# Four-layer graph network on one core: layer 2's normalised rows made and turned one batch earlier, three small steps moved

## The chip, the cores and the metric

One core of a Trainium2 chip runs the whole computation as one launch. The metric is the device time of one execution in microseconds (us). The kernel before was timed in three runs; the median counts.

## The reference, cut to what matters

`x` has 32 batches of 512 rows with 128 features, and `adj` is one 512 x 512 matrix shared by all batches. Four layers follow each other; each normalises every row, clips it at zero and adds what it computes to `x`:

```python
# layer 0: a softmax over adj's non-zero pattern mixes the rows
h = jnp.maximum(_layernorm(x), 0.0); x = x + _L0_gnn_ref(h, adj, ...)
# layer 1: two hops along adj, relu(stack @ Theta1 + bias)
h = jnp.maximum(_layernorm(x), 0.0); x = x + _L1_gnn_ref(h, adj, adj, ...)
# layer 2 (h is H, and weights = adj * adj)
features = relu(H @ psi_w + psi_b)
messages = einsum('nm,bnd->bmd', weights, features)
hidden = relu(concat(messages, H) @ phi1_w + phi1_b)
x = x + hidden @ phi2_w + phi2_b
# layer 3: exp(8 * tanh(score / 8)) * adj, rows divided by their sums, times h, times v
h = jnp.maximum(_layernorm(x), 0.0); x = x + _L3_gnn_ref(h, adj, q, k, v)
```

## The kernel before, in words

`x` stays in SBUF for the whole run, as 16 pairs of batches (`xt[q]`, q = 0 to 15; batch n is half b of pair q = n // 2). Every layer needs the statistics of each row, then the normalised rows (`h`), then these rows turned so that features lie on the partitions (`hT`).

**Statistics.** `stats_steps` (L239) of one pair issues four `bn_stats` on VectorE (L245), one square root on ScalarE (L252 or L254), and a reciprocal and a small multiply on VectorE (L256, L257). `low_stats` (L261) does the same without ScalarE: four `bn_stats` (L269) and four small operations on GpSimd (L271 to L274).

**Normalised and turned rows in layers 2 and 3.** `chunk(layer, m)` (L1076) makes the normalised rows of batch m with four ScalarE activations (L1089). `turn_half(layer, m)` (L1092) turns 32 x 32 blocks of them on VectorE (L1098) into one half of the tile `hb`, a ring of two buffers that both layers share; with the second half of a pair it also issues four 128 KB stores from SyncE to a DRAM tile `d` (L1104). `fetch(layer, q)` (L1107) loads the pair back from `d` as `hT` (512 KB, L1112, a ring of four); SyncE's queue is in order, so a fetch waits there until the four stores have landed.

**Order.** The order of instructions on TensorE, VectorE, ScalarE and GpSimd is the order of the source: a manual schedule covers these four engines, and DMAs that are held keep their place on SyncE's queue. So the place of a call in the source is its place in each engine's queue.

**Layer 0's last round and layer 1.** `round0(r)` (L794) handles pairs A = 2r and C = 2r + 1 of layer 0. It spreads the statistics of earlier pairs (`own_a`, `own_c`, L846) between its matrix products. In the last round (r = 7) `own_c` is pair 13. `layer1` (L950) handles two pairs per round: `split_up` makes high, low and mid parts of `h` (`moving_parts`, L418: high on ScalarE L420, low on GpSimd L421, mid on VectorE L422), `first` multiplies them with `adj` (`p_x1T`, L405, copied by ScalarE at L407), `weighed` and `mix` follow. In its first round it makes the statistics of pairs 14 and 15 (L1051, L1062). `more(step)` (L1352) places the first chunks, turns, fetches and features of layer 2 at the end of layer 1; step 7 is the last.

**Layer 2** is the first loop of `layers_2_and_3` (L1252), over n = 0 to 31. In iteration n: `messages(n)` (`p_msgT`, L1138, 12 matmuls), a chunk of layer 3 from n = 7 on, a chunk of layer 2 for batch n + 6, the copy of `p_msgT` out of PSUM by VectorE (L1276), `biased(n)` on GpSimd (L1167), `features(n + 2)` (`p_feat`, L447, from `hT`; then VectorE L1126, ScalarE L1127 and L420, GpSimd L421, VectorE L422), `hidden(n - 1)` (`p_phi`, L1147 and L1148, then ScalarE L1149), then the turns of the chunks that the iteration before made, `updated(n - 2)` (`p_l`, L447, then VectorE L1157, and for the second batch of a pair its statistics), and in even iterations a fetch for the batches n + 4 and n + 5. Two more statistics (pairs 14 and 15) are made at n = 2 and 3.

**Layer 3** is the second loop. `key_parts(n)` (ScalarE L426, VectorE L427, GpSimd L428) must precede `queries(n)` (`p_query`, L1183, then ScalarE L432 and VectorE L433, L434). `scores(n)` makes four tiles `ex` with a tanh and an exp each on ScalarE (L1211, L1203) and a multiply by the mask, alternately on VectorE and GpSimd (L1205). `attended(n - 1)` (`p_av`, L1232) uses the tiles of the batch before.

The lines below are the source that the change touches:

Of the kernel before, what the change touches and what calls it, by code (L numbers as in the profile page):

```python
# [29 lines left out]
def kernel(  # L30
# [38 lines left out]
    B, N, D = x.shape  # L69
# [3 lines left out]
    NQ = B // 2  # L73
# [138 lines left out]
    def ln_stats(q, low=False):  # L212
        for _ in stats_steps(q, low):
            pass
# [46 lines left out]
    def low_stats(q):  # L261

        st = stats.tile([P, NT, 2, 3], F32, tag="bn", name=f"bn_{q}", bufs=4)
        sd = stats.tile([P, NT, 2], F32, tag="sd", name=f"sd_{q}", bufs=4)
        rs = stats.tile([P, NT, 2], F32, tag="rs", name=f"rs_{q}")
        sh = stats.tile([P, NT, 2], F32, tag="sh", name=f"sh_{q}")
        for k in range(NT):
            b, t = divmod(2 * k, NT)
            nc.vector.bn_stats(st[:, k].rearrange("p e s -> p (e s)"),  # L269
                               xt[q][:, b, t : t + 2, :].rearrange("p t f -> p f t"))  # L270
        nc.gpsimd.tensor_scalar(sd, st[:, :, :, 2], 1.0 / (D * LOW**2), EPS / LOW**2, OP.mult, OP.add)  # L271
        nc.gpsimd.tensor_scalar(sh, st[:, :, :, 1], -1.0, None, OP.mult)
        nc.gpsimd.tensor_tensor(rs, sd, minus_half, OP.pow)
        nc.gpsimd.tensor_mul(sh, sh, rs)  # L274
        shift[q] = sh.rearrange("p k e -> p (k e)")
        scale[q] = rs.rearrange("p k e -> p (k e)")
# [202 lines left out]
    def go(steps, n=99):  # L479
        for _ in range(n):  # L480
            if next(steps, steps) is steps:
                return
# [311 lines left out]
    def round0(r):  # L794
# [48 lines left out]
        more = r + 1 < NQ // 2  # L843
        nothing = iter(())
        stats_a, stats_c = ahead.get(A + 5, nothing), ahead.get(C + 5, nothing)
        own_a, own_c = own.pop(A - 2, nothing), own.pop(C - 2, nothing)  # L846
        for i, _ in enumerate(products(f"l0_{r}", by_token, sums["att"], now, evict,
                                          ORDER if r else ORDER0)):
            if r == 0:
# [100 lines left out]
    def layer1(more, square):  # L950
# [68 lines left out]
        for r in range(NQ // 2):  # L1019
            A, C = 2 * r, 2 * r + 1  # L1020
            last = r == NQ // 2 - 1
            if r == 0:
                first(A, 1)
                split_up(C, 0)
                split_up(C, 1)
                straighten(C)
            else:
                split_up(A, 1)
                straighten(A)
                mix(r - 1, 0)  # L1030
                normalised(C, NT)
                turn(C, 1)
                mix(r - 1, 1)
                normalised(C)
                turn(C)
                mix(r - 1, 2)
                split_up(C, 0)
                go(square, r > 3)
                mix(r - 1, 3)
                split_up(C, 1)  # L1040
                first(A, 1)
            weighed(A, 0)
            weighed(A, 1)
            if last:
                more(0)
            go(square, r > 2)
            first(C, 0)
            normalised(A + 2, NT)
            if last:
                more(1)  # L1050
            ln_stats(A - 2) if r else go(own[NQ - 2])  # L1051
            first(C, 1)
            if last:
                more(2)
            if r:
                straighten(C)
            split_up(A + 2, 0)
            normalised(A + 2)
            go(square, r > 3)
            weighed(C, 0)  # L1060
            weighed(C, 1)
            ln_stats(C - 2) if r else go(own[NQ - 1])  # L1062
            go(square, r > 3)
            turn(A + 2)
            first(A + 2, 0)
            if r == 0:
                normalised(C + 2, 0)
# [8 lines left out]
    def chunk(layer, m):  # L1076


        q, b = divmod(m, 2)
        if layer == 3 and m % 4 == 0:  # L1080
            h = wide_tile(f"h3_{m}")
            halves_h.update({(3, m + i): tiles(h[:, i]) for i in range(4)})
        elif layer == 2 and b == 0:
            h = normed_tile(q)
            halves_h.update({(2, m + i): h[:, i] for i in range(2)})
        h = halves_h[layer, m]
        for t in range(NT):
            i = b * NT + t
            nc.scalar.activation(h[:, t, :], xt[q][:, b, t, :], AF.Relu,  # L1089
                                 bias=shift[q][:, i : i + 1], scale=scale[q][:, i : i + 1])  # L1090
# [16 lines left out]
    def fetch(layer, q):  # L1107

        if q < NQ:
            hT = hTs[layer, q] = feature_major(f"hT{layer}_{q}")  # L1110
            tc.keep_in_program_order(
                nc.sync.dma_start(hT.rearrange("p i b n -> p (i b n)"), dh[layer, q].rearrange("j c i e -> (j c) (i e)")))  # L1112
# [38 lines left out]
    def updated(n):  # L1151

        if not 0 <= n < B:
            return
        q, b = divmod(n, 2)
        p = projected(f"p_l2_{n}", (columns(msgT[n // 4][:, n % 4]), phi2))
        nc.vector.tensor_add(xt[q][:, b], p, xt[q][:, b])  # L1157
        if b == 1 and q == NQ - 1:
            low_stats(q)
        elif b == 1:  # L1160
            ln_stats(q, low=True)

    def biased(n):
# [88 lines left out]
    def layers_2_and_3():  # L1252


        later, ready = iter(range(B)), []

        def ahead_of_3():
            m = next(later, B)
            if m < B:
                chunk(3, m)  # L1260
                ready.append((3, m))

        def turn_ready(now):
            for layer, m in now:
                turn_half(layer, m)

        mask_of = adjT_d.rearrange("(a b c) w -> b a c w", a=NT, c=QR)
        for n in range(B):
            p = messages(n)
            now, ready = ready, []  # L1270
            if 7 <= n < B - 1:
                ahead_of_3()
            if n + 6 < B:
                chunk(2, n + 6)
                ready.append((2, n + 6))
            nc.vector.tensor_scalar(msgT[n // 4][:, n % 4], p, UP, None, OP.mult)  # L1276
            biased(n)
            features(n + 2)
            if n == B - 1:
                queries(0)  # L1280
            hidden(n - 1)
            turn_ready(now)
            updated(n - 2)
            if n == 0:
                fetch(2, 2)
            elif n % 2 == 0 and n + 4 < B:
                fetch(2, n // 2 + 2)
            if n in (2, 3):
                ln_stats(NQ - 4 + n)
            if n == 12:  # L1290
                weights_of_3()
            if n == 20:
                adjTx.append(matrix_tile("adjTx"))
            if n >= 20 and n % 2 and n < 28:
                i = (n - 20) // 2
                tc.keep_in_program_order(nc.sync.dma_start(adjTx[0][:, i, :], mask_of[i]))
            if n in (26, 28, 30):
                fetch(3, (n - 26) // 2)
            if n in (29, 30):
                key_parts(n - 29)  # L1300
        hidden(B - 1)
        mapped(0)
        updated(B - 2)
        updated(B - 1)
        for n in range(B):
            last = n == B - 1
            queries(n + 1)
            key_parts(n + 2)
            if last:
                attended(n - 2, NT // 2)  # L1310
            else:
                scores(n)
                if n == B - 2:
                    attended(n - 1, 0, NT // 2)
                    mapped(n + 1)
                    scores(n + 1)
                    continue
            attended(n - 1)
            mapped(n + 1)
            if n % 2:  # L1320
                turn_ready(ready)
                ready = []
            elif n:
                ahead_of_3()
            if n % 2 == 0:
                fetch(3, n // 2 + 3)
        attended(B - 1, width=1)
# [24 lines left out]
    def more(step):  # L1352

        if step == 0:
            chunk(2, 0)
        elif step == 1:
            chunk(2, 1)
            turn_half(2, 0)
        elif step == 2:
            turn_half(2, 1)  # L1360
        elif step == 3:
            fetch(2, 0)
            chunk(2, 2)
        elif step == 4:
            turn_half(2, 2)
            chunk(2, 3)
        elif step == 5:
            turn_half(2, 3)
            features(0)
            chunk(2, 4)  # L1370
        elif step == 6:
            fetch(2, 1)
            features(1)
            turn_half(2, 4)
            chunk(2, 5)
        elif step == 7:
            turn_half(2, 5)

    next_layer = layer1(more, made_square)
    for r in range(NQ // 2):  # L1380
# [42 lines left out]
```

## Time and profile before

| quantity | value |
|---|---|
| median of 3 runs (lowest, highest) | 929.79 us (928.28, 930.12) |
| the profiled execution's own time | 931.19 us |
| its span, first to last instruction | 929.3 us |
| busy in the span: TensorE / VectorE / ScalarE / GpSimd | 906.4 / 668.5 / 527.7 / 488.0 us |
| mean granted TensorE clock | 0.996 of full speed |
| layer 2 in the span (first `p_msgT` to last `p_msgT` starts) | 452.28 us to 661.47 us |

The profiled execution is one of the program's executions; 1.9 us of its time lie outside the span. All durations below come from it. In the profile PE is TensorE's matrix multiply, PEld its weight load, DVE VectorE, ACT ScalarE, POOL GpSimd and SPq SyncE's queue, which issues the DMAs. In a line of the timeline the first number is the start from the beginning of the span, the second the length, both in us; xN says how many instructions are merged; a bracket at the end gives the idle time of the engine before it and what ended that.

### The profile page before, as it was taken

Reading aid. Unit: us, or ns where it says so; the run is one execution under the profiler, and the core shown is the slowest. Engines: PE = TensorE matmul, PEld = TensorE weight load, DVE = VectorE, ACT = ScalarE, POOL = GpSimd, SP = SyncE. Lnnn points to the kernel's source line nnn. Section 1 sums busy time; section 2 is a strip of 40 time slices with the busy share of each in tenths; the row PEclk is TensorE's granted clock in tenths of the full one; section 3 lists DMA queues with packets and bytes.
Section 4 is the critical chain, followed back from the end, with each engine's and each line's share of the span. In section 5 each row is a group of like instructions: output and inputs, shape, how many; then the busy total and the mean of one; then the engine's idle time right before and its main releaser. Section 6 shows DMA issues by size and latency. Waiting matters only on the chain.

```text
span 929.3 us, 15172 instructions
## 1 busy us (share of the span) xinstructions
PE 906.4 (98%) x5433; PEld 775.1 (83%) x5433; DVE 668.5 (72%) x1348; ACT 527.7 (57%) x1156; POOL 488.0 (53%) x435
## 2 busy tenths in 40 slices
PE   8999999999999999999998999999999999999998
PEld 4899999988888888888876766767789999999998
DVE  8888886666665665666575666666788888887775
ACT  5864553343452353344645776775487777766663
POOL 5968999732132245422444444444465665555553
PEclk9999999999999999999998999999999999999999
DMA  9255643113213302312312334346412232222111
GB/s 254 63 166 167 175 115 112 46 47 91 68 42 116 93 24 68 91 45 93 92 52 84 93 112 137 98 132 172 121 30 74 73 98 80 80 80 80 59 35 46
DMA packets 83915, 86.06 MB, mean 93 GB/s; under 512 B 6784, under 2 KB 74624, under 8 KB 83840
## 3 DMA queue, kind: packets, MB, share of 16 engines
q1 hardware_dynamic: 83552, 84.57, 31.8%
q8 instruction: 43, 0.70, 0.3%
q10 hardware_dynamic: 288, 0.52, 0.2%
q14 instruction: 32, 0.26, 0.1%
HBM read 44.17 MB, written 40.89 MB: 92 GB/s over the span
## 4 chain that ended last, share of the span: by engine, by line
PE 80%; DVE 5%; DMA 4%; POOL 4%; ACT 4%; issue 2%; SPq 1%; DVEq 0%; POOLq 0%; ACTq 0%
PE p_av L1232 12%; PE p_l L1003 10%; PE p_x1T L405 9%; PE p_score L1210 9%; PE p_w L447 6%; PE p_msgT L1138 4%; PE p_l_c L393 3%; PE p_l L999 3%; PE p_hv L447 3%; PE p_l_d L393 2%; PE p_g L447 2%; PE p_query L1183 2%; PE p_l_a L393 2%; ACT h L1089 2%; PE p_feat L447 2%
## 5 line engine op out<-in xcount | busy, mean ns | idle before, releaser
L421 POOL TENSOR_TENSOR low_feat<-feat,high_feat 128x512 fp32r<-128x512 f32 x32 | 56.5, 1767 | 131.9 <-ACT high_feat L420 131.4
L1232 PEld LDWEIGHTS p_av<-hv,ex 128*128 128x128 f32 x1024 | 119.2, 191 | 2.7
L1232 PE MATMUL p_av<-hv,ex 128*128 128x129 f32 x1024 | 119.4, 274 | 0.0
L285 ACT ACTIVATE h<-x,sh,rs 128x128 f32<-128x128 f32 x256 | 102.8, 483 | 12.5 <-DVE sh L257 11.5
L1205 DVE TENSOR_TENSOR ex<-ex,adjTx 128x512 f32<-128x512 f32 x64 | 82.5, 1289 | 34.9 <-ACT ex L1203 33.1
L1205 POOL TENSOR_TENSOR ex<-ex,adjTx 128x512 f32<-128x512 f32 x64 | 99.4, 1572 | 7.1 <-issue 4.2
L1089 ACT ACTIVATE h<-x,sh,rs 128x128 f32<-128x128 f32 x256 | 102.9, 484 | 0.0
L428 POOL TENSOR_TENSOR key<-key 128x512 fp32r<-128x512 f32 x32 | 50.3, 1570 | 94.4 <-DVE key L427 41.7
L421 POOL TENSOR_TENSOR low_h<-h,high_h 128x512 fp32r<-128x512 f32 x32 | 47.1, 1481 | 79.0 <-ACT high_h L420 78.8
L245 DVE BATCH_NORM_STATS2 bn<-x 128x6 f32<-128x256 f32 x244 | 85.8, 415 | 0.0
L407 ACT ACTIVATE x1T<-p_x1T 128x512 f32<-128x512 f32 x32 | 19.0, 594 | 106.8 <-PE p_x1T L405 106.8
L1203 ACT ACTIVATE ex<-ex 128x512 f32<-128x512 f32 x128 | 78.9, 651 | 0.0
L1211 ACT ACTIVATE ex<-p_score 128x512 f32<-128x512 f32 x128 | 74.0, 605 | 1.4 <-PE p_score L1210 1.3
L422 DVE SCALAR_TENSOR_TENSOR mid_feat<-feat,high_feat 128x512 fp32r<-128x512 f32 x32 | 24.4, 764 | 55.4 <-ACT high_feat L420 55.4
L432 ACT ACTIVATE high_query<-p_query 128x512 fp32r<-128x512 f32 x32 | 19.2, 600 | 73.1 <-PE p_query L1183 73.1
L974 POOL COPY hs<-hT 128x512 f32<-128x512 f32 x32 | 19.2, 630 | 79.0 <-DMA hT<-d_hT 78.9
L254 ACT ACTIVATE sd<-bn,eps 128x8 f32<-128x8 f32 x46 | 13.9, 302 | 64.5 <-DVE bn L245 61.4
L1210 PE MATMUL p_score<-low_query,key 128*128 128x512 f32 x128 | 50.4, 394 | 0.0
L1210 PE MATMUL p_score<-high_query,key 128*128 128x512 f32 x128 | 50.4, 394 | 0.0
L1210 PE MATMUL p_score<-mid_query,key 128*128 128x512 f32 x128 | 50.4, 394 | 0.0
L447 PEld LDWEIGHTS p_feat<-psi,hT 128*128 128x128 f32 x256 | 33.4, 195 | 19.4 <-issue 11.3
L447 PE MATMUL p_w<-th,x1T 128*128 128x128 f32 x256 | 49.5, 275 | 0.0
(220 smaller groups left out, 2370.2 us busy)
## 6 DMA issues: line engine op xcount, KB each, us to landing
d<-hb SPq DMA_DIRECT2D x128, 128.0 KB, 2.4
hT<-d SPq DMA_DIRECT2D x32, 512.0 KB, 3.7
d_hT<-hb_hT SPq DMA_DIRECT2D x112, 128.0 KB, 2.4
hT<-d_hT SPq DMA_DIRECT2D x28, 512.0 KB, 3.3
x<-in_x_dram SPq DMA_DIRECT2D x32, 256.0 KB, 5.3
out_dram<-x SPq DMA_DIRECT2D x31, 256.0 KB, 2.3
adjT_d<-adj_squares SPq DMA_DIRECT2D x4, 256.0 KB
adj_crossed<-in_adj_dram SPq DMA_DIRECT2D x4, 256.0 KB
```

Of the source, the lines that this page charges most:

```text
L245: nc.vector.bn_stats(st[:, k].rearrange("p e s -> p (e s)"), xt[q][:, b, t : t + 2, :].rearrange("p t f -> p f t"))
L285: nc.scalar.activation(h[:, b, t, :], xt[q][:, b, t, :], AF.Relu, bias=shift[q][:, i : i + 1], scale=scale[q][:, i : i + 1])
L405: nc.tensor.matmul(p, right[part][:, blk(t)], left[part][:, t, :], start=(t == 0 and part == 0), stop=(t == NT - 1 and part == 2))
L421: nc.gpsimd.tensor_sub(low, x, high.bitcast(F32))
L447: nc.tensor.matmul(p[:, blk(t)], hT(t), w, start=(i == 0), stop=(i == len(terms) - 1))
L1003: nc.tensor.matmul(p, adj_parts[part][:, t, blk(i)], w[r][part][:, t, :], start=False, stop=(part == 2 and t == NT - 1), skip_group_check= ...
L1089: nc.scalar.activation(h[:, t, :], xt[q][:, b, t, :], AF.Relu, bias=shift[q][:, i : i + 1], scale=scale[q][:, i : i + 1])
L1203: nc.scalar.activation(ex[:, t, :], ex[:, t, :], AF.Exp, scale=8.0)
L1205: eng.tensor_mul(split(ex[:, t, :]), split(ex[:, t, :]), crossed(mask[:, t, :]))
L1210: nc.tensor.matmul(p, keys[n][i][:, t, :], query[n][i], start=(i == 0), stop=(i == 2))
L1211: nc.scalar.activation(crossed(ex[:, t, :]), split(p), AF.Tanh, scale=UP / (8.0 * math.sqrt(D)))
L1232: nc.tensor.matmul(po[:, i, : D + 1], ex[:, t, blk(i0 + i)], hv[:, t, :], start=(t == 0), stop=(t == NT - 1))
```

## The change

Four things move; no arithmetic is added or removed.

1. Statistics of pair 13 leave layer 0's last round and go to layer 1's first round, just ahead of those of pair 14.
2. In layer 2, the chunk of batch n + 7 (instead of n + 6) is made in iteration n, the one of batch 6 in step 7 ahead of the loop. The turns of what the iteration before made are placed directly after `messages(n)`, ahead of the copy of `p_msgT`, instead of after `hidden(n - 1)`. The fetches, apart from the first, sit in odd iterations, one iteration earlier than before.
3. `key_parts(2)` goes from layer 3's first iteration to the end of layer 2, ahead of `hidden(31)`.
4. `low_stats` of pair 15 goes from `updated(31)` to layer 3's second iteration.

```diff
-        own_a, own_c = own.pop(A - 2, nothing), own.pop(C - 2, nothing)
+        own_a, own_c = own.pop(A - 2, nothing), own.pop(C - 2, nothing) if more else nothing
...
-            ln_stats(A - 2) if r else go(own[NQ - 2])
+            if r:
+                ln_stats(A - 2)
+            else:
+                go(own[NQ - 3])
+                go(own[NQ - 2])
...
-        if b == 1 and q == NQ - 1:
-            low_stats(q)
-        elif b == 1:
+        if b == 1 and q < NQ - 1:
             ln_stats(q, low=True)
...
-        later, ready = iter(range(B)), []
+        later, ready = iter(range(B)), [(2, 6)]
...
             p = messages(n)
-            now, ready = ready, []
+            turn_ready(ready)
+            ready = []
             if 7 <= n < B - 1:
                 ahead_of_3()
-            if n + 6 < B:
-                chunk(2, n + 6)
-                ready.append((2, n + 6))
+            if n + 7 < B:
+                chunk(2, n + 7)
+                ready.append((2, n + 7))
...
             hidden(n - 1)
-            turn_ready(now)
             updated(n - 2)
             if n == 0:
                 fetch(2, 2)
-            elif n % 2 == 0 and n + 4 < B:
-                fetch(2, n // 2 + 2)
+            elif n % 2 and n + 5 < B:
+                fetch(2, n // 2 + 3)
...
+        key_parts(2)
         hidden(B - 1)
...
-            key_parts(n + 2)
+            if n:
+                key_parts(n + 2)
+            if n == 1:
+                low_stats(NQ - 1)
...
             turn_half(2, 5)
+            chunk(2, 6)
```

## The prediction, made before the changed kernel ran

> **What bounds the kernel now.** I read the page first, then who waited for whom on TensorE, then windows by stage, then the timeline where TensorE stood still. The page's parts 1 and 2 show TensorE busy throughout, with one dip in slice 21 and in the granted clock a slice later:
>
> ```profile
> PE 906.4 (98%) x5433; PEld 775.1 (83%) x5433; DVE 668.5 (72%) x1348; ACT 527.7 (57%) x1156; POOL 488.0 (53%) x435
> ```
>
> The windows view says where the missing 23 us are (columns: length, then busy us of PE, PEld, DVE, ACT, POOL, then clock):
>
> ```profile
> 200.00:452.00 252.00, 252.00 (x1475) 219.69 (x1474) 154.52 (x279) 105.06 (x239) 79.88 (x78) 1.00 0.26 72
> 467.54:661.47 193.93, 180.77 (x892) 134.53 (x890) 129.50 (x257) 126.92 (x289) 88.98 (x85) 0.98 0.39 112
> 637.45:656.32 18.87, 18.87 (x98) 14.40 (x97) 11.94 (x23) 10.44 (x23) 9.59 (x10) 1.00 0.55 159
> ```
>
> Layer 1 (first row) has no idle TensorE at all. Layer 2 from messages(3) to messages(31) (second row) has 193.93 - 180.77 = 13.16 us, and a lowered clock. The third row is three iterations of layer 2 without a stall: 6.29 us each, the pace TensorE can hold. The waits of TensorE name one cause:
>
> ```profile
> PE p_feat L447 <- DMA hT<-d: 13.1, 10, 3.6
> ```
>
> Ten times `features` stood before a fetch that had not landed. The worst, on TensorE's timeline:
>
> ```profile
> 488.62 1.10 PE L1138 MATMUL p_msgT<-sq_mid,mid_feat 128*128 128x512 f32 x4
> 493.34 2.05 PE L447 MATMUL p_feat<-psi,hT 128*128 128x128 f32 x8 [3.62 <-DMA hT<-d]
> 495.18 1.91 PE L1147 MATMUL p_phi<-hT,phi 128*128 128x512 f32 x2
> 502.64 1.05 PE L447 MATMUL p_feat<-psi,hT 128*128 128x128 f32 x8
> ```
>
> After 3.62 us of idling the same eight matmuls took 2.05 us, later 1.05 us: half clock. Why are fetches late again and again? This part of the timeline is a stretch of the loop where neither TensorE nor a DMA is waited for:
>
> ```profile
> 507.71 1.42 DVE L245 BATCH_NORM_STATS2 bn<-x 128x6 f32<-128x256 f32 x4
> 509.17 0.30 ACT L252 ACTIVATE sd<-bn,eps_low 128x8 f32<-128x8 f32 x1 [2.78 <-DVE bn L245]
> 509.38 3.17 ACT L1089 ACTIVATE h<-x,sh,rs 128x128 f32<-128x128 f32 x8
> 509.82 0.68 DVE L1276 TENSOR_SCALAR msgT<-p_msgT 128x512 f32<-128x512 f32 x1
> 512.46 0.61 ACT L1127 ACTIVATE feat<-feat 128x512 f32<-128x512 f32 x1
> 514.43 1.30 DVE L1098 STREAM_TRANSPOSE hb<-h 128x512 f32<-128x512 f32 x2
> 519.58 1.30 DVE L1098 STREAM_TRANSPOSE hb<-h 128x512 f32<-128x512 f32 x2
> 521.38 1.40 DVE L245 BATCH_NORM_STATS2 bn<-x 128x6 f32<-128x256 f32 x4
> ```
>
> VectorE and ScalarE hand work to each other: statistics, square root, eight activations of the two chunks, then feat, its high part, the mid part, two turns, an add; then a lighter iteration. From statistics to statistics, two iterations, it takes 521.38 - 507.71 = 13.67 us, against TensorE's 2 x 6.29 = 12.58. The turns, hence stores and fetches, are paced by this loop. So two things bound layer 2: the loop's 13.67 us, and a fetch that leaves no spare time behind the turn.
>
> Two small idles lie elsewhere: 1.16 us before `mid_h` at 187.75, and
>
> ```profile
> 678.18 0.50 PE L1183 MATMUL p_query<-key,qk_parts 128*128 128x512 f32 x1 [1.20 <-POOL key L428]
> ```
>
> **What the Trainium skill says.** "TensorE: Matmul & The Clock Gate", section "What's actually happening", puts the clock at half after an idle window of about 3.4 us and back at full after about as much activity. The trace agrees: only the 3.62 us idle is followed by half clock; idles up to 1.61 us are not. "DMA: Bandwidth & Descriptors", section on the anatomy of one DMA, gives 2.0 us fixed plus bytes / 436 GB/s: an estimate of 2.3 us for a store and 3.2 for a fetch; the page's rows say 2.4 and 3.7 here (the measured ones are used). "SBUF — State Buffer", section "Who interferes with whom", says a VectorE instruction with two SBUF inputs and a GpSimd one lock each other out for a whole instruction. The trace agrees: the mid part takes 0.69 us, but 1.84 at 475.07, beside GpSimd's low part.
>
> **Part by part.**
>
> *Layer 2, what goes.* Stalled, messages(3) to messages(31) takes 193.93 us. Unstalled it is 27 x 6.29 + 5.39 (iteration 30 has no features; 656.08 to 661.47) = 175.22. Difference 18.71 us: 13.14 of idling, 3.2 of half clock (iteration 6 took 13.12 us, 6.83 too many, of which 3.62 are idle), and 2.3 of restarting after gaps.
>
> *Does the fetch come in time?* Chunk and turn are an iteration earlier. Before, a second-half turn sat in iteration 2k - 4 after the mid part; now it opens iteration 2k - 5, for the same features(2k) in 2k - 2. That is 6.3 us for the iteration plus 4.6 from VectorE's opening of an iteration to its turn (509.82 to 514.43): almost 11 us earlier, against a lateness of at most 3.62. Counted forward: turns 1.3, eight stores at 0.43 (the median row) 3.5, landing 2.4, fetch 3.7, together 11 us; VectorE opens an iteration 3.8 us behind TensorE (509.82 against messages at 506.06) and features come 2.9 us into one (508.95), so there are 3 x 6.29 + 2.9 - 3.8 = 18 us. The stall goes, and about 7 us are spare. Buffers: fetch of pair k takes the buffer of k - 4, last read by hidden in the iteration before; free.
>
> *What is late next: the loop.* The order of instructions shows each pair of turns passing the add and, in odd iterations, the statistics. The turns at 514.43 now come after the small multiply that ends the statistics (509.74 + 0.17), where ScalarE is busy with the eight activations until 512.46. VectorE's path there is 509.9 + 1.22 (turns) + 0.6 (copy) + 0.6 (feat) = 512.4: hidden, with 0.1 us to spare. The other turns, at 519.58, go ahead of the lighter iteration's copy and stay on the path. Loop: 13.67 - 1.22 = 12.45, under 12.58 by 0.13. So TensorE becomes the bound; but the cover is thin. If a lock of 1.84 - 0.69 = 1.15 us hits one mid part in every second loop, the loop averages 13.0, 0.45 too slow in each of the nine double iterations with both layers' chunks (n = 7 to 24): 4 us, less what the parts are ahead of TensorE's need: the relu of hidden at 513.64 is ready at 514.31 and used by `p_l` at 517.86, 3.5 us, of which I count 2. I take 1.0 us for this; bounds 0 and 4.
>
> *SyncE's queue.* Turns of layer 3 and layer 2 now complete a pair in the same odd iteration: eight stores instead of four and four, then the fetch. The next turns write the same `hb` buffers, so they wait for these stores. With the new order the light iteration's turns come at about 515.0 (mid 513.82, add 514.43), 5.1 after the others at 509.9; on to the next ones it is 12.45 - 5.1 = 7.3, and 0.6 more for the second buffer: 7.9 us. The last of the eight stores lands 0.7 + 3.5 + 2.4 = 6.6 after the turn began. No wait, 1.3 us spare.
>
> *Start of the loop.* Chunk(2,6) keeps its place on ScalarE (it merely changes iteration); chunk(2,7) is added ahead of feat(2) in ScalarE's 2.61 us of idling before 456.93: 1.64 us, hidden. Without that cover it would cost that.
>
> *Pair 13's statistics.* Four `bn_stats`, reciprocal and multiply leave the path before `mid_h`: VectorE is free at 185.2 (end of `x` from p_l_e) instead of 186.5. GpSimd's low part may still lock it until 186.6; gain 0.5 to 1.3, I take 1.1. Given back in layer 1: pair 14's square root now waits for pair 13's reciprocal and then its own `bn_stats`; ScalarE's square root moves from 200.20 to about 200.5 + 0.4 + 1.4 = 202.3, and behind it is queued the copy of `p_x1T` (200.85), which `p_w` needs at 202.66. New 202.6 + 0.6 = 203.2: a stall of 0.6. Net +0.5; bounds -0.5 and +1.2.
>
> *key_parts(2) and low_stats(15).* The 1.20 us go, but ScalarE's key part now sits before hidden(31)'s relu (0.1 to 0.3 us), and `p_av` at 681.30 had the last GpSimd tile of batch 0 ready at 681.53 only, used 0.3 us later: what starts earlier there is ScalarE's tanh and exp, by 0.3 to 0.6. In the next iteration `low_stats` puts 2.3 us of GpSimd (0.20 + 0.24 + 1.67 + 0.20) ahead of batch 1's tiles, which end at 687.5 against a use at 689.7. Net +0.3; bounds -0.8 and +1.2.
>
> *Sum:* 18.7 - 1.0 + 0.5 + 0.3 = 18.5. Of the profiled execution: 931.19 - 18.5 = 912.7. It lies 1.4 us over the median, so 929.79 - 18.5 = 911.3.
>
> **Rivals.**
> 1. *TensorE sets layer 2's pace* (as summed), 911.3; 908.5 to 913.5. For: hand-over loop shorter than 12.58, fetch 7 us early.
> 2. *The loop still sets the pace*, at 13.0 to 13.4 through locks: 9 x 0.4 to 0.8, less 2, is 1.6 to 5.2 us in place of case 1's allowance of 1.0: 912 to 915.5, about 914. For: 0.13 us of margin. Against: the stretch shown already has GpSimd's low part in it, with mid first.
> 3. *Features still wait for fetches* (the change doesn't do what it says), because SyncE's queue holds them behind the other stores: gains only the first stall, 6.8, and about nothing else: 923. Against: 7 us spare.
> 4. *Slower:* `hb` buffers come free late. If stores crowd, the turn blocks VectorE, with copy and feat queued behind it, and the loop is 12.45 plus the wait. To eat the 18.5 us in nine double iterations it must reach 12.58 + (18.5 + 1 + 2) / 9 = 15.0: a last store landing 7.9 + 2.5 - 4.2 = 6.2 us after its issue. At 6.7 us the loop is 15.5: 9 x 2.9 - 2 - 1 = 23 over case 1, 934. Against: the stores of `hb` landed in 2.0 to 3.4 us.
>
> **Numbers.** Chances: case 1 0.64, case 2 0.25, case 3 0.06, case 4 0.05. The range runs from 908.0 (all stalls gone, the small parts at their best: 18.7 + 1.2 + 1.2 = 21.1, 908.7, and some scatter) to 916.5 (case 2's end); it leaves out cases 3 and 4. A measurement of this kernel tells about 0.2% (1.9 us) from no change: faster is cases 1 to 3 and a little less, 0.93; same 0.02; slower 0.05.
>
> **What would show it.** Right: no `p_feat` wait for hT; no half clock near 490; messages 6.29 us apart from 467 to 661; turns between the multiply L257 and the copy of `p_msgT`. A new wait at the copy of `p_x1T` or `p_w` near 201.5, and a shorter one at the third batch's `p_query`. Wrong: pitch above 12.7 us per two iterations with TensorE waiting for low or mid feat (case 2), turns waiting for stores (case 4), or a half clock without idling.

## The result, and the profile after

| | before | after |
|---|---|---|
| median of the runs, timed together (lowest, highest) | 929.95 us (928.28, 930.22; 4 runs) | 912.73 us (912.55, 912.96; 4 runs) |
| ratio after / before, 95% interval | | 0.9819 (0.9802 to 0.9836) |
| profiled execution: time, span | 931.19, 929.3 us | 912.96, 911.2 us |
| mean granted TensorE clock | 0.996 | 1.000 |

The forecast was 911.3 us (908.0 to 916.5); for the profiled execution 912.7, which came out at 912.96. That the sum comes within 0.3 us there is luck. By the medians the kernel gained 17.2 us and not 18.5; the profiled execution of before was 1.2 us slower than the median of its runs. Nor do all terms of the sum hold; the sections below say which.

The first line of part 1 of the page of after:

```profile
PE 901.1 (99%) x5432; PEld 774.2 (85%) x5433; DVE 669.7 (74%) x1348; ACT 527.5 (58%) x1156; POOL 485.6 (53%) x435
```

The same instructions are there. TensorE is 5.3 us less busy, for no stretch runs at half clock and few matmuls restart after a gap; its idle time fell from 23 to 10 us. The windows of after (columns as before: length, busy us of PE, PEld, DVE, ACT, POOL, clock, share of the DMA engines, GB/s), first messages(3) to messages(31), then three unstalled iterations:

```profile
465.83:643.20 177.37, 176.03 (x891) 133.20 (x890) 132.70 (x255) 126.01 (x286) 88.59 (x86) 1.00 0.41 117
618.94:637.80 18.86, 18.86 (x99) 14.40 (x98) 12.67 (x25) 12.33 (x26) 9.67 (x10) 1.00 0.55 167
```

177.37 in place of 193.93: 16.56 of the 18.2 us come from here. It is still 2.15 us more than 27 iterations of 6.29 and one of 5.39. VectorE is 3.2 us *busier* than before in this stretch (132.70 against 129.50), though it does nearly the same work (255 instructions against 257). The waits of TensorE in after (us in total, times, longest):

```profile
PE p_l L447 <- ACT msgT L1153: 1.3, 2, 0.7
PE p_av L1234 <- POOL ex L1207: 0.8, 1, 0.8
...
PE p_w L447 <- ACT x1T L407: 0.3, 1, 0.3
```

The ten waits of `features` for `hT` are gone, and so are those at `mid_h` and `p_query`. Three small ones are new: `p_l` for the relu of `hidden`, `p_w` for the copy of `p_x1T`, and `p_av` for GpSimd's tile. (Waits in the first 20 us of the run, and one of 0.3 us that before has too, are left out here.) Now the loop between VectorE and ScalarE, on VectorE's timeline, two iterations from statistics to statistics:

```profile
501.44 1.41 DVE L245 BATCH_NORM_STATS2 bn<-x 128x6 f32<-128x256 f32 x4
503.22 0.20 DVE L256 RECIPROCAL rs<-sd 128x8 f32<-128x8 f32 x1 [0.37 <-ACT sd L252]
503.46 0.17 DVE L257 SCALAR_TENSOR_TENSOR sh<-bn,rs 128x8 f32<-128x8 f32 x1
503.64 1.30 DVE L1102 STREAM_TRANSPOSE hb<-h 128x512 f32<-128x512 f32 x2
504.87 0.65 DVE L1279 TENSOR_SCALAR msgT<-p_msgT 128x512 f32<-128x512 f32 x1
505.44 0.68 DVE L1130 TENSOR_TENSOR feat<-p_feat,psib 128x512 f32<-128x512 f32 x1
507.55 1.80 DVE L422 SCALAR_TENSOR_TENSOR mid_feat<-feat,high_feat 128x512 fp32r<-128x512 f32 x1 [1.43 <-ACT high_feat L420]
...
513.76 0.69 DVE L422 SCALAR_TENSOR_TENSOR mid_feat<-feat,high_feat 128x512 fp32r<-128x512 f32 x1 [1.42 <-ACT high_feat L420]
514.37 0.69 DVE L1161 TENSOR_TENSOR x<-p_l,x 128x512 f32<-128x512 f32 x1
514.97 1.42 DVE L245 BATCH_NORM_STATS2 bn<-x 128x6 f32<-128x256 f32 x4
```

The turns stand right behind the small multiply, as forecast, and ScalarE's eight activations (503.10 to 506.18) cover them. Yet the loop takes 514.97 - 501.44 = 13.53 us, not 12.45: one of the two mid parts takes 1.80 us in place of 0.69. GpSimd's low part of the same features says why:

```profile
507.54 1.27 POOL L421 TENSOR_TENSOR low_feat<-feat,high_feat 128x512 fp32r<-128x512 f32 x1 [4.11 <-ACT high_feat L420]
...
513.86 1.72 POOL L421 TENSOR_TENSOR low_feat<-feat,high_feat 128x512 fp32r<-128x512 f32 x1 [3.22 <-ACT high_feat L420]
```

Both engines wait for the same high part. At 507.54 GpSimd is 0.01 us ahead: its instruction runs undisturbed in 1.27 us, and VectorE's, which takes 0.69 alone, ends 0.54 us after it: VectorE was locked out for nearly all of GpSimd's instruction. At 513.76 VectorE is 0.10 us ahead: its instruction takes 0.69 and GpSimd's 1.72. How far VectorE has fallen behind (start of its copy of `p_msgT` less start of the same `messages`, worked out from the trace, us), and the mid part made in that iteration:

| iteration n | 6 | 8 | 10 | 12 | 14 | 16 | 20 | 24 |
|---|---|---|---|---|---|---|---|---|
| mid part | 1.83 | 1.80 | 1.81 | 1.81 | 0.69 | 0.69 | 0.69 | 0.69 |
| VectorE behind by | 7.10 | 7.49 | 8.43 | 9.36 | 9.58 | 8.16 | 7.62 | 7.08 |

While every loop has its lock, VectorE falls behind by 0.94 us in two iterations (13.52 - 12.58), until TensorE has to wait, at n = 13 and 15:

```profile
535.15 1.16 PE L447 MATMUL p_l<-phi,msgT 128*128 128x128 f32 x8 [0.63 <-ACT msgT L1153]
...
548.85 1.16 PE L447 MATMUL p_l<-phi,msgT 128*128 128x128 f32 x8 [0.72 <-ACT msgT L1153]
```

From n = 13 on VectorE is ahead by 0.045 us each time, no lock comes any more, and it catches up by 0.27 us in two iterations. The loop from n = 12 also holds a small operation that is done once for layer 3 (`qk_parts`, 0.30 us on VectorE); it takes 13.71 us.

My theory after this (theory L below): the place of the turns gave the gain, by taking them out of the hand-over loop; who wins the lock decides the 2.15 us left. The rivals: the earlier chunks and fetches gave the gain, since the fetch was issued too late (rival F), and the two stalls have another cause.

### The profile page after: what moved, and what is told of

Read it like the earlier page. It is cut to its first block, busy times and chain, and to the rows that moved or that the text cites. A ratio compares the mean times of both kernels' runs of the same rounds, so it can differ in the third digit from the quotient of the medians.

```text
span 911.2 us, 15170 instructions
## 1 busy us (share of the span) xinstructions
PE 901.1 (99%) x5432; PEld 774.2 (85%) x5433; DVE 669.7 (74%) x1348; ACT 527.5 (58%) x1156; POOL 485.6 (53%) x435
## 4 chain that ended last, share of the span: by engine, by line
PE 92%; ACT 3%; DVE 3%; POOL 1%; issue 0%; DMA 0%; DVEq 0%; POOLq 0%; ACTq 0%
PE p_av L1234 12%; PE p_l L1003 10%; PE p_x1T L405 9%; PE p_score L1212 9%; PE p_msgT L1142 9%; PE p_w L447 6%; PE p_l_c L393 4%; PE p_l L999 3%; PE p_l_a L393 3%; PE p_l_d L393 3%; PE p_g L447 3%; PE p_l L447 3%; PE p_hv L447 3%; PE p_feat L447 3%; PE p_phi L1151 3%; PE p_phi L1152 3%
## 5 line engine op out<-in xcount | busy, mean ns | idle before, releaser
L421 POOL TENSOR_TENSOR low_feat<-feat,high_feat 128x512 fp32r<-128x512 f32 x32 | 53.9, 1686 | 115.8 <-ACT high_feat L420 111.7
L1207 DVE TENSOR_TENSOR ex<-ex,adjTx 128x512 f32<-128x512 f32 x64 | 80.4, 1259 | 35.7 <-ACT ex L1205 34.0
L422 DVE SCALAR_TENSOR_TENSOR mid_feat<-feat,high_feat 128x512 fp32r<-128x512 f32 x32 | 28.9, 904 | 44.3 <-ACT high_feat L420 44.3
L447 PE MATMUL p_w<-th,hs 128*128 128x128 f32 x256 | 49.4, 275 | 0.0
```

Source lines behind the costliest of these rows:

```text
L421: nc.gpsimd.tensor_sub(low, x, high.bitcast(F32))
L447: nc.tensor.matmul(p[:, blk(t)], hT(t), w, start=(i == 0), stop=(i == len(terms) - 1))
L1207: eng.tensor_mul(split(ex[:, t, :]), split(ex[:, t, :]), crossed(mask[:, t, :]))
```

## Experiments

Where each kernel spends its time (us, worked out from the starts of instructions in the profiled executions; messages(0) to messages(3) is 15.25 to 15.30 in all):

| kernel | start to first `p_x1T` | to messages(0) | messages(3) to (31) | messages(31) to end | span |
|---|---|---|---|---|---|
| before | 184.19 | 268.09 | 193.93 | 267.85 | 929.3 |
| after | 183.61 | 266.97 | 177.37 | 267.98 | 911.2 |
| layer 2 undone | 183.59 | 266.96 | 193.30 | 267.77 | 926.9 |
| turns only | 183.72 | 266.94 | 176.38 | 267.80 | 910.1 |
| chunks and fetches only | 183.57 | 266.95 | 186.20 | 268.02 | 920.0 |
| layer 2 only | 186.28 | 267.64 | 177.36 | 267.80 | 914.3 |
| low part first | 183.58 | 267.15 | 192.95 | 270.20 | 929.2 |
| mid part first | 184.81 | 267.17 | 175.17 | 267.85 | 910.3 |
| pair 13 undone | 184.04 | 267.65 | 177.37 | 267.75 | 912.1 |
| key parts, pair 15 undone | 183.97 | 266.95 | 177.38 | 267.75 | 911.3 |
| two moves corrected | 183.58 | 266.35 | 177.37 | 266.89 | 909.5 |
| both corrected and mid first | 183.83 | 266.60 | 175.17 | 267.03 | 907.9 |

The first column varies by up to 2.7 us, in waits near the start that the edits do not touch (`p_incl` L530 waits 0.3 us in after and 1.3 in layer 2 only). So small effects are read from the columns, not from the totals. Each ratio below is to the kernel before, timed on the same chip.

**Layer 2 undone.** The layer 2 hunks of the diff reversed, the other three parts kept.

> The changed kernel with the layer 2 part alone put back as it was: turns after hidden(n - 1), chunks for batch n + 6, fetches in even iterations. My theory (the whole gain but 1 to 2 us is layer 2's): 928 to 929 us, ten waits of features for hT with about 13 us in all, one stretch at half clock. Rival (the small moves matter more, or the parts help each other): under 925.

Measured: 929.39 us median against 929.31, ratio 0.9998 (0.9991 to 1.0006). Ten waits for `hT` of 13.0 us in all are back. The median lies a little above the expected 928 to 929. The whole measurable gain is layer 2's; what the other parts bring is inside this measurement's uncertainty.

**Turns only.** The turns stay directly after `messages(n)`; chunks and fetches go back to where they were before.

```diff
-        later, ready = iter(range(B)), [(2, 6)]
+        later, ready = iter(range(B)), []
...
-            if n + 7 < B:
-                chunk(2, n + 7)
-                ready.append((2, n + 7))
+            if n + 6 < B:
+                chunk(2, n + 6)
+                ready.append((2, n + 6))
...
-            elif n % 2 and n + 5 < B:
-                fetch(2, n // 2 + 3)
+            elif n % 2 == 0 and n + 4 < B:
+                fetch(2, n // 2 + 2)
...
             turn_half(2, 5)
-            chunk(2, 6)
```

> The changed kernel with the turns directly after messages, but chunks for batch n + 6 and fetches in even iterations as before. Theory L (the hand-over loop of VectorE and ScalarE was the bound, and the place of the turns shortens it): the turn comes 4.6 us earlier than before, which leaves 18.0 - 6.3 = 11.7 us up to the features against 1.3 + 4 x 0.43 + 2.4 + 3.7 = 9.1 needed, so no wait for hT: 912 to 914 us, two iterations in 12.6 to 13. Rival F (the fetch was late because it was issued late, and the 6.3 us of the earlier chunk are what removed that): stalls for hT come back in most pairs, 918 to 925.

Measured: 912.07 us, ratio 0.9811 (0.9795 to 0.9828), as good as after with all of it. TensorE's only wait for a fetch in layer 2:

```profile
PE p_feat L447 <- DMA hT<-d: 0.5, 1, 0.5
```

This agrees with theory L, but does not prove it alone: the new place also makes each turn 4.6 us earlier, more than the 3.62 us by which the latest fetch was late. The next kernel separates the two. The one wait (0.48 us, at 551.71) shows that the spare time behind the fetch is nearly used up.

**Chunks and fetches only.** The counterpart: chunks for batch n + 7 and fetches in odd iterations, as in after.

```diff
-            turn_ready(ready)
-            ready = []
+            now, ready = ready, []
...
             hidden(n - 1)
+            turn_ready(now)
```

> The changed kernel with chunks for batch n + 7 and fetches in odd iterations, but the turns after hidden(n - 1) as before. Theory L: the loop of VectorE and ScalarE stays at 13.67 us per two iterations, 1.09 over TensorE; from n = 7 to 24 that is 9 x 1.09 = 9.8, less about 4 us of lead that is used up first: 5.8 over a kernel without stalls in layer 2 (910.6), so 916 to 918 us, with TensorE waiting for mid feat, low feat or the relu of hidden, hardly for hT. Rival F: being 6.3 us earlier against a lateness of 3.6 at most is enough, 911 to 913.

Measured: 921.96 us, ratio 0.9912 (0.9898 to 0.9927). No wait for `hT`; instead:

```profile
PE p_l L447 <- ACT msgT L1153: 7.3, 7, 1.9
```

Here the fetches are 6.3 us earlier and in time, and still more than half of layer 2's gain is missing: rival F fails and theory L stands. The loss is larger than I expected: 186.20 - 175.17 = 11.0 us in layer 2, not 5.8. From n = 20 to 26 three loops without any lock take 13.5 us each, which is the loop with turns on its path. The rest was added between n = 11 and 17: by three locked mid parts and by a stretch of half clock that is shown in the last section.

Together: in layer 2 the earlier chunk and fetch alone save 193.30 - 186.20 = 7.1 us, the turns' place alone 16.9, both 15.9. Once the turns are out of the loop, fetching earlier adds nothing; it even costs 1.0 us. Of the loops with both layers' chunks, three were locked in after (n = 8, 10 and 12) and one with turns only (n = 10).

**Low part first.** VectorE copies one column of the high part ahead of its mid part, which is meant to let GpSimd start first in every iteration.

```diff
-        feats[n] = three(f"feat_{n}")
-        moving_parts(feat, *feats[n])
+        high, low, mid = feats[n] = three(f"feat_{n}")
+        nc.scalar.activation(high, feat, AF.Copy, scale=DOWN)
+        nc.gpsimd.tensor_sub(low, feat, high.bitcast(F32))
+        nc.vector.tensor_copy(tick, high[:, 0:1].bitcast(F32))
+        nc.vector.scalar_tensor_tensor(mid, feat, 1.0 / UP, high.bitcast(F32), OP.mult, OP.subtract)
```

> The changed kernel, with one column of the high part copied by VectorE (an instruction of about 0.1 us) between the high part and the mid part of the features, so that GpSimd's low part always starts first and locks the mid part in every iteration. Lock theory (the 13.5 us per two iterations at n = 8 to 14 are 12.4 plus one lock of 1.1): two locks make 14.6 us, against TensorE's 12.58; 9 x 2.0 less 4 of lead is 14 us over a layer 2 without stalls (910.6), so 922 to 927 us. Rival (the two stalls at n = 13 and 15 have another cause, the order of VectorE's work at the hand-over): 912 to 914.

Measured: 931.37 us, ratio 1.0019 (1.0008 to 1.0030): the whole gain is lost, with no wait for a fetch. The copy delays VectorE by only 0.07 us, so in five iterations between n = 4 and 12 the mid part still went first, by 0.02 to 0.03 us, and took 0.68 to 0.69; from n = 13 on GpSimd went first each time. VectorE in that steady stretch:

```profile
571.93 0.15 DVE L1136 COPY tick<-high_feat 128x1 f32<-128x1 f32 x1 [1.36 <-ACT high_feat L1134]
572.00 1.79 DVE L1137 SCALAR_TENSOR_TENSOR mid_feat<-feat,high_feat 128x512 fp32r<-128x512 f32 x1
```

The loop takes 14.65 us (messages(18) at 567.24, messages(20) at 581.89), as expected (14.6); the copy itself adds some 0.07 us per iteration. The time was 4 us worse than my range, for I let the locks count only up to n = 24: they hold TensorE up to n = 30, and 2.2 us more go in layer 3's start.

**Mid part first.** GpSimd reads one column of the mid part before it makes the low part, so VectorE always starts first.

```diff
-        feats[n] = three(f"feat_{n}")
-        moving_parts(feat, *feats[n])
+        high, low, mid = feats[n] = three(f"feat_{n}")
+        nc.scalar.activation(high, feat, AF.Copy, scale=DOWN)
+        nc.vector.scalar_tensor_tensor(mid, feat, 1.0 / UP, high.bitcast(F32), OP.mult, OP.subtract)
+        nc.gpsimd.tensor_copy(tick, mid[:, 0:1].bitcast(F32))
+        nc.gpsimd.tensor_sub(low, feat, high.bitcast(F32))
```

> The changed kernel, with GpSimd reading one column of the mid part before it makes the low part, so that the mid part always goes first and nothing locks VectorE there. Lock theory: loop under 12.58 us throughout, no wait of p_l for the relu of hidden, 910.3 to 911.2 us. Against it: the low part ends 0.3 to 0.4 us later (its smallest slack before its use is 0.68 us), which may show as new waits at the low features: 912 to 913. Rival (another cause): the stalls at n = 13 and 15 stay, 912.5 to 913.

Measured: 912.01 us, ratio 0.9806 (0.9791 to 0.9821). The window of layer 2, then VectorE and GpSimd for one iteration:

```profile
467.28:642.45 175.17, 175.17 (x891) 133.57 (x890) 129.22 (x255) 126.78 (x286) 79.00 (x114) 1.00 0.42 118
```

```profile
506.80 0.69 DVE L1135 SCALAR_TENSOR_TENSOR mid_feat<-feat,high_feat 128x512 fp32r<-128x512 f32 x1 [1.42 <-ACT high_feat L1134]
```

```profile
507.63 0.18 POOL L1136 COPY tick<-mid_feat 128x1 f32<-128x1 f32 x1 [4.65 <-DVE mid_feat L1135]
507.76 1.28 POOL L1137 TENSOR_TENSOR low_feat<-feat,high_feat 128x512 fp32r<-128x512 f32 x1
```

TensorE is busy for all 175.17 us: 2.20 less than in after and within 0.05 of the 175.22 that my prediction called unstalled. The low part ends later and nobody waits for it. The lock was the whole residue in layer 2. The total is 0.7 us lower, not 2.2, and above the 910.3 to 911.2 expected: this execution reached the first `p_x1T` 1.2 us later than after did. One loop (n = 12, with `qk_parts`) took 13.6 us, against the expectation of less than 12.58 throughout; TensorE did not wait for it.

**Pair 13's statistics undone.** The first two hunks of the diff reversed.

> The changed kernel with pair 13's statistics put back into layer 0's last round. As the two traces are read: the wait of 1.16 us before mid_h comes back, the wait of 0.49 us at p_w goes, net 0.6 to 1.2 us lost: 913.3 to 913.9. Rival (the trace of before and of after differ there by chance, as 0.55 us of the difference are there before mid_h): 912.7, no difference.

Measured: 913.68 us, ratio 0.9827 (0.9813 to 0.9842). From the first `p_x1T` to messages(0) it takes 267.65 us, after 266.97: the part is worth 0.7. The wait that is back is shorter than the 1.16 us of before, whose instructions are the same up to there; so it seems to vary between executions:

```profile
PE p_x1T L405 <- DVE mid_h L422: 0.7, 1, 0.7
```

**Key parts and pair 15's statistics undone.** The hunks of parts 3 and 4 reversed.

> The changed kernel with the third batch's key parts and pair 15's statistics put back. The two traces differ by 0.2 us to the disadvantage of the new places: 912.5, with p_query waiting 1.1 us for key again and p_av not waiting for ex. As forecast (0.3 us gained by the new places): 913.0. Neither can be told from the other by time alone; the waits can.

Measured: 912.85 us, ratio 0.9818 (0.9803 to 0.9832). `p_query` waits 1.1 us for the key again, `p_av` does not wait. From messages(31) to the end: 267.75, after 267.98. These two parts give nothing together.

**Layer 2 only.** Parts 1, 3 and 4 reversed.

> The kernel before with the layer 2 part alone. If the parts simply add: the changed kernel's 912.7 plus 1.2 to 1.7 us for pair 13's statistics, less 0.2 for the third batch's key parts and pair 15's statistics: 913.7 to 914.3 us. If they don't add (the start of layer 2 shifts the locks in it): anything from 911 to 916, with another number of iterations that take over 7 us.

Measured: 914.26 us, ratio 0.9831 (0.9816 to 0.9845). Layer 2 takes 177.36 us, with the same locks in the same iterations as in after. The parts add.

**Two moves corrected.** What parts 1 and 4 give back, taken out:

```diff
                 go(own[NQ - 3])
+            first(C, 1)
+            if not r:
                 go(own[NQ - 2])
-            first(C, 1)
...
-            if n == 1:
-                low_stats(NQ - 1)
...
                 scores(n)
+                if n == 1:
+                    low_stats(NQ - 1)
```

> The changed kernel with two of its small moves corrected: pair 14's statistics behind the second p_x1T and its copy instead of ahead of it, and pair 15's statistics behind the scores of batch 1 instead of ahead. If the two new waits that the changed kernel shows are what they cost, p_w's 0.31 us and p_av's 0.57 to 0.77 us go: 0.8 to 1.1 us less, 911.7 us. Rival (something else on these engines is late by as much there): 912.5.

Measured: 911.27 us, ratio 0.9803 (0.9785 to 0.9822). Against after, 0.6 us go between `p_x1T` and messages(0), 1.1 behind messages(31). Both waits are gone. By the medians, 1.46 us are gained, more than the 0.8 to 1.1 expected.

**Both corrected and mid part first.**

> The same two corrections, and GpSimd held until the mid part of the features is made, so that nothing locks VectorE there. Layer 2 from messages(3) to messages(31) at TensorE's 175.2 us instead of 177.4, and the two small waits gone: 912.7 - 2.2 - 0.9 = 909.6 us. Rival (the gains don't add, the low part's later end shows somewhere): 911.

Measured: 909.70 us (909.59 to 910.28, 5 runs), ratio 0.9787 (0.9769 to 0.9806): 3.0 us better than the changed kernel's median, and in layer 2 TensorE is again at 175.17 us. The sum is the expected one; its parts are not: by the medians mid part first adds 1.57 us to the two corrections here. Of its 2.20 in layer 2, some 0.6 are lost again in the other columns, 0.1 to 0.25 us in each; that is not explained.

## Why the prediction was right, point by point

**Layer 2's stall (18.7 us): right.** Mid part first has no stall left and takes 175.17 us where before took 193.93: 18.76. Its half clock share can be seen by itself too: of the nine executions of before that were timed beside the last two kernels, two show a mean clock of 1.000 and took 927.04 and 927.34 us; the other seven, at 0.996, took 929.81 to 931.08. That is some 3 us, against my 3.2. No trace of such an execution was kept, so it is not shown that nothing else differed.

**The fetch comes in time: right, with less to spare.** No `features` waited. SyncE's queue in after, for the pair that features(14) reads:

```profile
510.60 4.67 SPq L1108 DMA_DIRECT2D d<-hb  x8
517.64 0.34 SPq L1116 DMA_DIRECT2D hT<-d  x1
```

The fetch landed after 3.2 us, at 520.85; features(14) came at 525.46. That is 4.6 us to spare, not 7: VectorE was 7.4 us behind TensorE here, not 3.8. What I had wrong is what the fetch needed: turns only shows that the 4.6 us of the turns alone suffice.

**The buffers of SyncE's queue (1.3 us spare): mis-sized, harmless.** Eight stores took 4.67 us to issue here, and 3.71 to 4.82 in the loops up to n = 25; I counted 3.5. The fetch of 517.64 marks the landing of the last four; the next turn into their buffer came 0.17 us later, in other loops up to 1.4. No turn waited, so case 4 did not come; its point was nearer than I said.

**The loop (12.45 us): right without a lock, wrong for n = 8 to 13.** In mid part first VectorE catches up from 6.38 to 5.76 us behind over ten iterations, 0.12 per two: 12.58 - 0.12 = 12.46. In after it took 12.31 from n = 16 on, where no lock comes, but 13.51 to 13.71 in the three loops from n = 8 to 13. This is the term of the sum that was mis-sized: I took "1.0 us for this", with one lock "in every second loop"; it came in every loop for a while and not at all later, and cost 2.2. So case 2's mechanism ruled for these six iterations and case 1's for the rest. "Against: the stretch shown already has GpSimd's low part in it, with mid first" was a poor argument. Mid was first there by 0.04 us, and locks do occur in before (n = 2 and 3).

**Pair 13's statistics (+0.5): right.** 0.7 in the runs. The give-back was foreseen at 0.6, as a wait at `p_w` behind the copy of `p_x1T`; taking it out brought 0.6 (0.31 of idling, the rest in the restart after it). The gross gain was then 1.3, forecast 1.1.

**Key parts and pair 15's statistics (+0.3): wrong, about 0.** The 1.2 us at `p_query` went. But I put `low_stats` at 2.3 us of GpSimd, ahead of tiles with 2.2 us to spare. On GpSimd's timeline of after:

```profile
665.37 1.17 POOL L271 TENSOR_SCALAR sd<-bn 128x8 f32<-128x8 f32 x1
...
666.83 1.67 POOL L273 TENSOR_TENSOR rs<-sd,minus_half 128x8 f32<-128x8 f32 x1
...
668.74 2.99 POOL L1207 TENSOR_TENSOR ex<-ex,adjTx 128x512 f32<-128x512 f32 x2
```

It took 3.4 us: the first small operation 1.17 instead of 0.20. So the tile was late and `p_av` waited. Placed behind the tiles, as in the corrected kernel, the part saves 267.75 - 266.89 = 0.9 us. That the long first operation, too, was a lock (VectorE has two-input work beside it) is only argued.

**The total.** 18.2 us between the profiled executions: 16.56 from layer 2, 1.1 from `p_x1T` to messages(0), 0.6 from ahead of it, less 0.1 behind messages(31). Not all of it was shown to belong to the change. The stretch ahead of the first `p_x1T` varies between executions, and so, it seems, does the wait at `mid_h`: of the 1.1, 0.7 is pair 13's and 0.45 is that wait, which was 1.16 us in before and 0.7 in the kernel with pair 13's statistics put back. Without these two, 17.2 us are left, the difference of the medians. So two shares that the change did not earn, 1.0 us together, made up for most of the 1.2 us by which the lock was undersized.

## What to carry to other kernels

A late transfer may be the end of a loop that is too slow, and then an earlier issue only buys time until the lag has grown; measure the loop's length against the bound's, and take work off its path. Where two engines wait for the same result and lock each other out, give them an order by a real dependency, with the engine first whose delay costs more: here VectorE, which was in the loop. A moved step's price is its length at the new place, beside new neighbours, not at the old one.

## What the hardware showed that I had not expected

**A lock decided by a hundredth of a microsecond.** The Trainium skill, "SBUF — State Buffer", section "Who interferes with whom", says that issue order decides which of VectorE and GpSimd is blocked. The traces agree. What they add is how thin the decision is: where GpSimd starts 0.011 or 0.012 us before VectorE, the mid part takes 1.80 to 1.84 us; where VectorE starts 0.042 to 0.099 before GpSimd, it takes 0.69. The same iterations are hit in after and in layer 2 only. The two outcomes are not equal: mid first costs the low part 0.45 to 0.55 us (1.72 to 1.82 for 1.27), low first costs the mid part 1.1. What sets these hundredths was not found.

**Half clock without a long idle.** On TensorE's timeline of chunks and fetches only:

```profile
553.07 1.47 PE L447 MATMUL p_l<-phi,msgT 128*128 128x128 f32 x8 [1.94 <-ACT msgT L1153]
554.19 2.05 PE L1142 MATMUL p_msgT<-sq_high,high_feat 128*128 128x512 f32 x4
556.05 1.62 PE L1142 MATMUL p_msgT<-sq_low,low_feat 128*128 128x512 f32 x4
557.50 1.09 PE L1142 MATMUL p_msgT<-sq_mid,mid_feat 128*128 128x512 f32 x4
```

The longest idle of this kernel's layer 2 is 1.94 us, and yet four matmuls after it took 2.05 us in place of 1.17; at 557.50 the clock was back. The Trainium skill, "TensorE: Matmul & The Clock Gate", section "What's actually happening", has the clock fall after at least one idle window of about 3.4 us, and says that the window runs freely. The second agrees with the traces. The granted clock was half from 553.78 to 557.19 us here, from 492.58 to 499.41 in before and from 489.90 to 496.72 in layer 2 undone: one or two times 3.41 us. Counted from the first change of the clock in each trace (7.65, 7.89 and 5.20 us), the first of these stretches begins after 160 times 3.4133 us, the other two after 142 times. The skill's other statement does not hold here: a window need not be idle throughout. Cut into these windows, the traces show (idle is the window's length less TensorE's busy time in it):

| kernel | window, us | idle in it | clock in the next |
|---|---|---|---|
| before | 489.17 to 492.58 | 2.86 us, 84% | 0.50 |
| chunks and fetches only | 550.37 to 553.78 | 1.94 us, 57% | 0.50 |
| layer 2 undone | 486.48 to 489.90 | 1.92 us, 56% | 0.50 |
| low part first | 592.39 to 595.80 | 1.55 us, 45% | 1.00 |
| before | 519.89 to 523.30 | 1.47 us, 43% | 1.00 |
| chunks and fetches only | 536.71 to 540.13 | 1.15 us, 34% | 1.00 |

No other window of layer 2, in any of the twelve traces, has more than 45% of idle at full clock. So the share of a window that had to be idle lies between 45% and 56% in these runs, an estimate, for the ends of matmuls are modelled. What counts is also where a gap falls: the 1.94 us lay inside one window, while another idle of this kernel, 1.87 us long and ended at 537.86, was divided between two and did nothing. My rule from before (only 3.62 us of idling) was too simple.
